# A perceiver kernel whose unit loop goes from three iterations to two, and whose constant rows are filled by transfers

## The chip, the cores and the metric

The kernel runs on one core of one Trainium2 chip, as a single launch. The metric is the device time in microseconds, median of several executions. The engines are named as in the profile: PE (TensorE matmuls) and PEld (its weight loads), DVE (VectorE), ACT (ScalarE), POOL (GpSimd), and SP (SyncE), whose queue issues nearly all DMAs.

## What is computed

The reference is a two-layer perceiver on a latent `x` of 32 batches x 64 tokens x 256, with a context of 32 x 1601 x 256:

```python
x = x + L0_xattn(layernorm(x), ctx, ...)         # 16 heads of 16, 1601 keys
x = x + L0_attn(layernorm(x), ...)               # self-attention over the 64 tokens
x = x + L0_ffn(layernorm(x), ...)                # half of the tokens, chosen by a gate
x = x + L1_xattn(layernorm(x), ctx, mask, ...)   # the same context, masked
x = x + L1_attn(layernorm(x), ...)               # quantized self-attention
x = x + L1_ffn(layernorm(x), ...)                # product-key lookup
```

Each cross-attention projects the whole context to keys and values, takes `softmax(q k^T)` per head, and multiplies by the values. The change concerns the two cross-attentions and the start of the kernel.

## The kernel before, in words

One long part, `stream`, does both cross-attentions and, between them, the small layers of layer 0. The last two layers of layer 1 come behind it and are not touched.

The stream is cut into 256 *units*, `u` = 0 to 255: two layers x 32 batches x four groups of four heads. The order of the instructions on every engine is the order in which the Python code issues them (a manual schedule), so it is written out by hand in the loop of L1408. A unit needs, in this order:

- `fetch(u)` (L1179): the four heads' keys come from a buffer in HBM (`kd`) into one of three SBUF tiles `kst`, by eight DMAs (nine in layer 1, with the mask's row). Numbers are kept as three bf16 parts in different rows of the tile; some rows hold constants: ones at `MAXR`, which -max of the queries multiplies, the mask at `MASKR`, zeros elsewhere. `fetch(u + 2)` is issued at the start of unit `u`, into the tile that unit `u - 1` read last. It also advances the delayed steps (`tick`) by one.
- `maxima(u)` (L1217): scores in natural layout, in four groups of 400 keys: matmuls `sp` (L1228, two PSUM banks a group), DVE's maxima `mx` (L1233); then -max, two small casts `mm`, four matmuls `rp` (L1248) that lay it along the tokens, and two ACT copies (L1253) into the query tile `qst`. It is a generator that stops after each group, after `mm` and after the copies.
- `probabilities(u, j)` (L1259), for seven tiles j of 256 keys (the last has 65): transposed scores less the maximum, matmuls `tp` (L1269), and exp on ACT into a tile `e` (L1274). `tp` has two PSUM banks, `e` has three buffers.
- `weighted(u, j, e)` (L1277): matmuls `acc` (L1284), probabilities times values; each is two instructions, 16 a tile, 8 for the last.

Beside the units run:

- `keys_values` (L1292): projections of later batches, about 1.8 batches ahead, in PSUM banks that alternate between keys (L1081) and values (L1109), twelve matmuls each, some 3.2 banks a unit. DVE adds the key bias into `kr` (L1087); ACT copies values out (L1114).
- `tick` (L997): delayed steps. Each call advances every pending one by one step, with at most two that are marked "work": the split of the context into two parts (`halved`: ACT `chi` L978, then POOL `clo`), the first cast of keys (ACT L1031, then POOL L1032 and L1033), two calls later the second (ACT L1038), then the store to `kd` (L1041, SP).
- `group_step` and `end_step`: one step each of queries, self-attention, the feed-forward layer, and of what follows a finished batch pair.

The before loop has three iterations a unit. With tiles `js` = (0, 1, 2), (3, 4), (5, 6):

```python
for i, js in enumerate(((0, 1, 2), (3, 4), (5, 6))):
    # two steps of maxima(u + 1) in the first and second iteration
    # weighted() of the tiles left from the iteration before
    # in the third: rp and the copies of -max of unit u + 1
    late = [(u, j, probabilities(u, j)) for j in js[:2]]
    # group_step, end_step, tick, then a bank of keys or values
    late += [(u, j, probabilities(u, j)) for j in js[2:]]
```

So -max of a unit is ready before the unit starts. At the start of the kernel, loads of the first context tiles, weights and biases are issued (L1338 on); the key bias's eight small DMAs go on ACT's queue (L268), all others on SP's. POOL sets the constant rows with memsets: two whole `kst` tiles and their rows of ones (L1351 to L1354), two whole `qst` tiles and rows of ones (L1355 to L1362). The first queries follow: DVE's statistics (L561), a small rsqrt on POOL (L199 to L193), normalization on DVE (L568).

Of the kernel before, what the change touches and what calls it, by code (L numbers as in the profile page):

```python
# [20 lines left out]
F32 = mybir.dt.float32  # L21
F32R = mybir.dt.float32r
BF16 = mybir.dt.bfloat16
# [38 lines left out]
class Kernel:  # L62
# [192 lines left out]
    def biases(self, wp, n, which):  # L255
        b = self.WNAMES[n][3]
        got = []
        for x in which:
            full = self.ins[b % x if n else b + x]
            if x == "v":  # L260
                got.append(self.load_row(wp, full, D, f"b{x}{n}"))
            elif x == "k":

                t = wp.tile([P, 2], F32, tag=f"bk{n}", name=f"bk{n}")
                with self.nc.allow_non_contiguous_dma(reason="a bias, once"):
                    for q, a, j in product(range(2), repeat=3):

                        (self.nc.sync if n else self.nc.scalar).dma_start(  # L268
                            t[64 * q + 2 * a + j : 64 * q + 64 : 4],
                            full.rearrange("(c q j a d) -> q j a d c", q=2, j=2, a=2, d=16)[  # L270
                                q, j, a
                            ],
                        )
                got.append(t)
            else:
                got.append(self.load_cols(wp, full, 2, f"b{x}{n}"))
        return got

    def stream_setup(self, wp, bg, bank):
# [41 lines left out]
        tri = bg.tile([P, P], F32, tag="oT", name="tri")  # L321
# [188 lines left out]
    def stream(self):  # L510
        nc, tc, ins = self.nc, self.tc, self.ins
        with ExitStack() as ctx:
# [6 lines left out]
            kq = pool("kq")  # L519
            kp_ = pool("kst")  # L520
            vp_ = pool("v")
            pt = pool("pt", 3)
            small = pool("s", 4)
            work = pool("w", 2)
            bg = pool("bg", 1)
# [72 lines left out]
            def queries(n, g):  # L598

                name = f"xa{n}"  # L600
                if g == 0 and n == 1:
                    self.load_natural(self.wq, ins[self.WNAMES[n][0]])
                xT = yield from normed(g, name)
                qp = project(None, self.wq, xT, f"{name}_qp{g}")
                qf = bg.tile([P, 2, 2 * P], F32, tag="qf", name=f"{name}_qf{g}")
                for oc in range(2):
                    nc.vector.tensor_scalar(
                        qf[:, oc, :], qp[:, oc, :], self.bq[n][:, oc : oc + 1],
                        0.25 if n else 1.0, ALU.add, ALU.mult,
                    )  # L610
# [12 lines left out]
                waiting[0] = True  # L623
                yield
                yield
                q = qring[g % 2]
                qh = halves(q)
                for a in range(2):
                    for r, rows, part in (
                        (a, FIRST, 0), (1 - a, FIRST, 2), (a, SECOND, 1), (1 - a, SECOND, 0),  # L630
                        (a, THIRD, 0), (1 - a, THIRD, 1),
                    ):
                        nc.sync.dma_start(
                            parity(qh[r, rows], a),
                            qd[part].rearrange("(j a d) n -> a d j n", a=2, d=16)[a],
                        )
                        if r != a:
                            yield

                nc.sync.dma_start(q[MAXR : P : 64], q[ZERO : P : 64])  # L640
                qsts[NG * n + g] = q
                yield

# [154 lines left out]
            def self0(g):  # L798
                xT = yield from normed(g, "sa0")
                rp = bank(f"sa0_rp{g}")  # L800
                for cc in range(2):
# [28 lines left out]
                def out(t, oT):  # L830
                    rp = bank(f"sa0_ro{g}_{t}")
                    for c in range(2):
                        nc.tensor.matmul(
                            rp[:NH, :P], self.basT[:, c, 3 * NH :], oT[:, c, :],
                            start=(c == 0), stop=(c == 1),
                        )
                    ro = bg.tile([NH, P], F32, tag="ro", name=f"sa0_rs{g}_{t}")
# [10 lines left out]
            def ffn0(g):  # L848
# [12 lines left out]

                def wide(tag, dt=F32):

                    home = dict(dg="oT", row="ro").get(tag, f"ff_{tag}")
                    return bg.tile([P, 2, NQ], dt, tag=home, name=f"ff0_{tag}{g}")


# [156 lines left out]
            def parted(i, x, quick):  # L1024
# [9 lines left out]
                if not quick:  # L1034

                    yield "wait"
                    yield "work"
                nc.scalar.copy(ks[:, 1, :, :m], upper(x))  # L1038
                yield "store"
                for b, k0, n, o in spans(i):  # L1040
                    nc.sync.dma_start(  # L1041
# [307 lines left out]


            for k in kring[:2]:  # L1351
                nc.gpsimd.memset(k, 0.0)
                for r in (MAXR, MAXR + 64):
                    nc.gpsimd.memset(k[r : r + 1], 1.0)  # L1354
            for q in qring:  # L1355
                nc.gpsimd.memset(q, 0.0)

                for a in range(2):
                    r = 64 * a + 32
                    nc.gpsimd.memset(  # L1360
                        q[r : r + 5].rearrange("p (j a) n -> p j a n", a=2)[:, :, a], 1.0
                    )  # L1362
# [4 lines left out]
            for i in range(6):  # L1367
# [4 lines left out]
            pad = bg.tile([P, 6, NKP - NK], BF16, tag="e", name="pad")  # L1372
            nc.vector.memset(pad, 0.0)
            nc.sync.dma_start(self.rows[:, NK:], pad[:NB, 0])

            for kd in kdring:
                nc.sync.dma_start(
                    kd.rearrange("s (c q) (h n) -> (q h) (s c) n", c=2, h=4)[:, :, NKE:],
                    pad[:, :, : NKP - NKE],
                )  # L1380
            steps = queries(0, 0)

# [17 lines left out]
            fetch(1)  # L1400
            banks_made(3)
            LEAD = 1.8
            for i, _ in enumerate(maxima(0)):
                if i < 4:
                    banks_made(1)
            groups.append((15, self.stream_setup(wp, bg, bank)))
            late = []
            for u in range(NU):  # L1408
# [14 lines left out]
                    groups.append((u + 15, queries(*divmod((u + 15) // 16, NG))))  # L1423
                if u + 2 < NU and u + 2 not in ksts:
                    fetch(u + 2)
                nat = maxima(u + 1) if u + 1 < NU else iter(())

                for i, js in enumerate(((0, 1, 2), (3, 4), (5, 6))):
                    for _ in range((2, 2, 0)[i]):
                        next(nat, None)  # L1430
                    for done in late:
                        weighted(*done)
                        if done[1] == 6 and done[0] % 8 == 7:
                            n, t = divmod(done[0] // 8, NT)
                            ends.append((n, t, finish(n, t)))
                            next(ends[-1][2])
                    if i == 2:
                        next(nat, None)
# [7 lines left out]
                    if i == 2:  # L1446
                        group_step()
                        if u % 2:
                            end_step()
                for _ in nat:  # L1450
                    pass
            for done in late:
                weighted(*done)
            ends.append((1, NT - 1, finish(1, NT - 1)))
# [973 lines left out]
```

## Time and profile before

| | |
|---|---|
| median of 3 executions | 3675.83 us (3670.55 to 3685.44) |
| the profiled execution | 3673.05 us |
| its span, first to last instruction | 3671.3 us |
| mean granted PE clock | 0.953 |
| first maxima matmul (unit 1's first) | 99.22 us (113.46 us) |
| last unit's first `acc` of its own tiles | 3134.24 us |
| PE waiting for DMA of `kst`, 300 to 3100 us | 16.2 us keys, 13.9 us mask rows |
| PE `acc` waiting for ACT `e`, 300 to 3100 us | 6.9 us |

The span is measured by the profiler; the device time of the same execution stands beside it. In a line of the timeline the columns are: start in us, duration, engine, line of the kernel, operation, tiles written and read, shapes, how many instructions were merged (x12), and in brackets how long the engine was idle before and what ended that. Matmuls overlap, so the time of a run of them is read from its start to the start of the next run. In a line of the waits: who waited, for whom, us in total, times, longest.

### The profile page before, as it was taken

The page shows a single profiled execution, that of the slowest core. Times are in us where ns is not written, and L with a number is a line of the kernel's source. Part 1 is how long each engine was busy: PE and PEld are TensorE (multiplying, and loading weights), DVE is VectorE, ACT ScalarE, POOL GpSimd, SP SyncE. Part 2 cuts the span into 40 slices and gives each one's busy share as a digit, 9 for nine tenths or more (in the row PEclk, how much of TensorE's full clock was granted, in tenths as well). Part 3 has the DMA queues.
Part 4 walks back from the last instruction along what each step waited for, and adds up shares of the span by engine and source line. Part 5 has one row for each costly group of instructions (what it writes and reads, how often), then busy time and mean ns, then how long its engine had stood idle before and what let it go on. Part 6 is the DMA issues. An engine that isn't in the chain of part 4 may idle for free. (4 is left out here: it accounts for less than half of the span.)

```text
span 3671.3 us, 148311 instructions
## 1 busy us (share of the span) xinstructions
PE 3325.6 (91%) x62993; PEld 2715.0 (74%) x63007; DVE 2430.4 (66%) x6165; ACT 2367.4 (64%) x4656; POOL 1837.9 (50%) x2121
## 2 busy tenths in 40 slices
PE   3799999999999999999999999999999998675698
PEld 3688788878778788778887878878788887332467
DVE  5556566666565566566567666656666666689879
ACT  2567666766766677667776767667677776154662
POOL 6455555554555555545555655555565563003246
PEclk9899999999999999999999999999999999886699
DMA  3888777776776777677787677677778887100000
GB/s 83 227 230 235 200 195 208 216 210 191 212 198 189 210 202 217 189 204 209 204 219 217 190 207 202 191 210 195 207 205 239 233 236 208 64 1 1 1 5 20
DMA packets 615336, 649.81 MB, mean 177 GB/s; under 512 B 127056, under 2 KB 579856, under 8 KB 598096
## 3 DMA queue, kind: packets, MB, share of 16 engines
q1 hardware_dynamic: 614288, 640.31, 63.5%
q8 instruction: 495, 8.11, 0.9%
q14 instruction: 169, 1.38, 0.1%
q10 hardware_dynamic: 384, 0.00, 0.0%
HBM read 468.30 MB, written 171.11 MB: 174 GB/s over the span
## 5 line engine op out<-in xcount | busy, mean ns | idle before, releaser
L1233 DVE TENSOR_REDUCE mx<-sp 128x1 f32<-128x400 f32 (+1 forms) x2048 | 1032.2, 566 | 314.1 <-PE sp L1228 313.6
L1274 ACT ACTIVATE e<-tp 128x512 f32<-128x512 f32 (+1 forms) x1792 | 931.7, 565 | 472.7 <-PE tp L1269 463.2
L979 POOL TENSOR_TENSOR clo<-raw,chi 128x512 fp32r<-128x512 f32 (+1 forms) x408 | 507.8, 1245 | 550.4 <-ACT chi L978 539.1
L1032 POOL TENSOR_TENSOR kr<-kr,ks 128x512 f32<-128x512 f32 (+1 forms) x406 | 459.0, 1130 | 620.9 <-ACT ks L1031 563.5
L1087 DVE TENSOR_SCALAR kr<-kp,bk 128x256 f32<-128x256 f32 (+1 forms) x832 | 356.5, 470 | 552.9 <-PE kp L1081 455.9
L1269 PE MATMUL tp<-qst,kst 128*128 128x64 bf16 (+1 forms) x13312 | 580.2, 195 | 18.3 <-ACT e L1274 15.9
L1284 PEld LDWEIGHTS acc<-e,v 128*17 128x17 f32 x26624 | 397.3, 98 | 217.7 <-issue 141.8
L1284 PE MATMUL acc<-e,v 128*17 128x64 f32 x26624 | 543.8, 223 | 14.7 <-ACT e L1274 11.5
L1269 PEld LDWEIGHTS <-kst 128*128 128x128 bf16 (+1 forms) x13312 | 463.1, 100 | 118.2 <-issue 25.7
L1109 PE MATMUL vp<-w_hi,chi 128*128 128x256 f32 (+1 forms) x1664 | 508.5, 306 | 33.2 <-DVE w_hi L222 30.0
L1109 PE MATMUL vp<-w_lo,chi 128*128 128x256 f32 (+1 forms) x1664 | 473.8, 285 | 0.4 <-DVE w_lo L223 0.3
L1109 PE MATMUL vp<-w_hi,clo 128*128 128x256 f32 (+1 forms) x1664 | 474.1, 285 | 0.0
L1033 POOL TENSOR_TENSOR ks<-kr 128x512 bf16<-128x512 f32 (+1 forms) x406 | 412.5, 1016 | 31.9
L1081 PE MATMUL kp<-chi,w_hi 128*128 128x256 f32 (+1 forms) x1664 | 370.8, 305 | 22.6 <-DVE w_hi L222 19.8
L1228 PE MATMUL sp<-kst,qst 64*64 64x400 bf16 (+1 forms) x4096 | 321.4, 351 | 76.6 <-DMA kst<-kd 39.2
L1114 ACT COPY v<-vp 128x512 f32<-128x512 f32 (+1 forms) x416 | 244.8, 589 | 206.5 <-PE vp L1109 203.4
L1081 PE MATMUL kp<-clo,w_hi 128*128 128x256 f32 (+1 forms) x1664 | 339.4, 286 | 16.5 <-POOL clo L979 15.6
L1109 PEld LDWEIGHTS vp<-w_hi,chi 128*128 128x128 f32 (+1 forms) x1664 | 314.4, 189 | 51.1 <-DVE w_hi L222 26.9
L1081 PE MATMUL kp<-chi,w_lo 128*128 128x256 f32 (+1 forms) x1664 | 337.1, 285 | 4.8 <-DVE w_lo L223 4.8
L1109 PEld LDWEIGHTS vp<-w_lo,chi 128*128 128x128 f32 (+1 forms) x1664 | 314.9, 189 | 1.7 <-DVE w_lo L223 0.9
L1109 PEld LDWEIGHTS vp<-w_hi,clo 128*128 128x128 f32 (+1 forms) x1664 | 314.2, 189 | 0.0
L978 ACT CAST chi<-raw 128x512 fp32r<-128x512 f32 (+1 forms) x410 | 249.7, 609 | 86.7 <-DMA raw<-in_ctx_dram 86.6
(725 smaller groups left out, 5191.5 us busy)
## 6 DMA issues: line engine op xcount, KB each, us to landing
kst<-kd SPq DMA_DIRECT2D x1024, 208.0 KB
kd<-ks SPq DMA_DIRECT2D x384, 384.0 KB
kst<-kd SPq DMA_DIRECT2D x1024, 104.0 KB
raw<-in_ctx_dram SPq DMA_DIRECT2D x379, 256.0 KB
qst<-xa_qd SPq DMA_DIRECT2D x192, 64.0 KB
kd<-ks SPq DMA_DIRECT2D x64, 108.0 KB
xa_qd<-xa_qs SPq DMA_DIRECT2D x16, 384.0 KB
raw<-in_ctx_dram SPq DMA_DIRECT2D x62, 72.0 KB
```

Of the source, the lines that this page charges most:

```text
L978: nc.scalar.copy(hi[:, :, :n], raw[:, :, :n])
L979: (nc.vector if i < 2 else nc.gpsimd).tensor_tensor(lo[:, :, :n], raw[:, :, :n], hi[:, :, :n].bitcast(F32), ALU.subtract)
L1032: eng.tensor_tensor(x, x, ks[:, 0, :, :m], ALU.subtract)
L1033: eng.tensor_tensor(ks[:, 2, :, :m], x, upper(x), ALU.subtract)
L1081: nc.tensor.matmul(kp[:, oc, :m], wk[w][:, cc, oc * P : (oc + 1) * P], x[:, cc, :m], start=(j == 0), stop=(j == 5),)
L1087: nc.vector.tensor_scalar(r[:, oc, :m], kp[:, oc, :m], self.bk[n][:, oc : oc + 1], None, ALU.add,)
L1109: nc.tensor.matmul(vp[:w_, i1, :], x[:, cc, o], wv[w][:, cc, :], start=(j == 0), stop=(j == 5),)
L1228: nc.tensor.matmul(sp[a][64 * j : 64 * j + 64, :n], q[r, h0 + 2 * j + a, tok], k[r, 2 * a + j, k0 : k0 + n], start=True, stop=True,)
L1233: nc.vector.tensor_reduce(mx[:, a, g : g + 1], sp[a][:, :n], AX.X, ALU.max)
L1269: nc.tensor.matmul(sp[:m, c, h, :], k[:, 2 * (h % 2) + h // 2, k0 : k0 + m], q[:, h0 + h, tok], start=True, stop=True,)
L1274: nc.scalar.activation(e[:m, :two], sp[:m, :two], AF.Exp)
L1284: nc.tensor.matmul(acc[32 * h : 32 * h + 17, slot, :], vs[b, c][:m, 4 * q4 + h, :], e[:m, c - 2 * i, h, :], start=(c == 0), stop=(c == NCH ...
```

## The change

The loop now has two iterations a unit. `maxima(u + 1)` does two of its steps in each; what is left of it, `rp` and the copies of -max, is kept as `own` and done in the first iteration of the unit that uses it, with a bank of keys or values between it and the unit's first scores. Tiles go out as 0, 1, then 2, 3 in the first iteration, 4, 5, 6 in the second, with banks between; `weighted` runs on four tiles (0 to 3) and three (4 to 6), so `e` has four buffers. `group_step`, `end_step` and `tick` (together `behind()`) are called four times a unit. In `parted`, the store of keys comes one tick later. To make room for the fourth buffer, the tiles `oT` and `ro` share buffers with others. At the start, the memsets of POOL are gone; a small tile of zeros and ones (`flat`) is written into the constant rows by ten DMAs on SP's queue, and the key bias's DMAs go on SP's queue too, behind the query weights. The rows of the query tiles that multiply the mask are zeros in layer 0, and are set to ones by two DMAs for the first two query groups of layer 1; the copy of zeros over the -max row is left out for the first two groups.

```diff
-                        (self.nc.sync if n else self.nc.scalar).dma_start(
+                        self.nc.sync.dma_start(
...
-            pt = pool("pt", 3)
+            pt = pool("pt", 4)
...
-                nc.sync.dma_start(q[MAXR : P : 64], q[ZERO : P : 64])
+                if n or g > 1:
+                    nc.sync.dma_start(q[MAXR : P : 64], q[ZERO : P : 64])
+                if n and g < 2:
+                    for a in range(2):
+                        r = MASKR + 64 * a
+                        nc.sync.dma_start(
+                            parity(q[r : r + 1], a),
+                            kring[0][MAXR : MAXR + 1, 0:1, : 2 * P].to_broadcast([1, 8, 2 * P]),
+                        )
...
-                rT = bg.tile([3 * NH, 2 * P], F32, tag="oT", name=f"sa0_rT{g}")
+                rT = bg.tile([3 * NH, 2 * P], F32, tag="kz", name=f"sa0_rT{g}")
...
                 nc.scalar.copy(ks[:, 1, :, :m], upper(x))
+                if not quick:
+                    yield "wait"
                 yield "store"
...
-            self.bk = self.biases(wp, 0, "k")
...
-            self.bq, self.bv = self.biases(wp, 0, "q"), []
+            self.bk, self.bq, self.bv = self.biases(wp, 0, "k"), self.biases(wp, 0, "q"), []
...
-            for k in kring[:2]:
-                nc.gpsimd.memset(k, 0.0)
-                for r in (MAXR, MAXR + 64):
-                    nc.gpsimd.memset(k[r : r + 1], 1.0)
-            for q in qring:
-                nc.gpsimd.memset(q, 0.0)
...
+            flat = bg.tile([P, 2, 512], BF16, tag="fraw", name="flat")
+            for x in range(2):
+                nc.vector.memset(flat[:, x], float(x))
+            def fill(rows, x):
+                rows = rows.rearrange("p h n -> p (h n)").rearrange("p (x n) -> p x n", n=512)
+                nc.sync.dma_start(
+                    rows, flat[: rows.shape[0], x : x + 1].to_broadcast(list(rows.shape))
+                )
+            for x in kring[:2] + qring:
+                for r in (32, 96):
+                    fill(x[r : r + 32 : 2], 0)
+            for k in kring[:2]:
+                fill(k[MAXR : P : 64], 1)
...
-                nat = maxima(u + 1) if u + 1 < NU else iter(())
-                for i, js in enumerate(((0, 1, 2), (3, 4), (5, 6))):
-                    for _ in range((2, 2, 0)[i]):
+                nat, own = maxima(u + 1) if u + 1 < NU else iter(()), nat
+                def some(*js):
+                    late.extend((u, j, probabilities(u, j)) for j in js)
+                def behind():
+                    banks[0] = 0
+                    group_step()
+                    end_step()
+                    tick()
+                def made_up_to(part):
+                    keys_values(LEAD + (u + part) / 4.0, 0.15)
+                for i in range(2):
+                    for _ in range(2):
                         next(nat, None)
                     for done in late:
                         weighted(*done)
...
-                    late = [(u, j, probabilities(u, j)) for j in js[:2]]
-                    banks[0] = 0
-                    group_step()
-                    end_step()
-                    tick()
-                    keys_values(LEAD + (3 * u + i + 1) / 12.0, 0.15)
-                    late += [(u, j, probabilities(u, j)) for j in js[2:]]
...
+                    late = []
+                    if i == 0:
+                        next(own)
+                        behind()
+                        made_up_to(1 / 3.25)
+                        some(0, 1)
+                        behind()
+                        made_up_to(2 / 3.25)
+                        some(2, 3)
+                    else:
+                        behind()
+                        some(4)
+                        made_up_to(1.0)
+                        some(5)
+                        behind()
+                        some(6)
```

More of the change, by code (lines that the diff above doesn't have):

```diff
@@ L320, in stream_setup @@
         nc.vector.tensor_tensor(self.eye, self.ident[:, :64], self.ident[:, 64:], ALU.add)
-        tri = bg.tile([P, P], F32, tag="oT", name="tri")
+        tri = bg.tile([P, P], F32, tag="e", name="tri")
         nc.gpsimd.memset(tri, 1.0)
@@ L836, in out @@
                         )
-                    ro = bg.tile([NH, P], F32, tag="ro", name=f"sa0_rs{g}_{t}")
+                    ro = bg.tile([NH, P], F32, tag="xT", name=f"sa0_rs{g}_{t}")
                     nc.scalar.copy(ro, rp[:NH, :P])
@@ L862, in wide @@
                 def wide(tag, dt=F32):
-                    home = dict(dg="oT", row="ro").get(tag, f"ff_{tag}")
+                    home = dict(dg="kz", row="kT").get(tag, f"ff_{tag}")
                     return bg.tile([P, 2, NQ], dt, tag=home, name=f"ff0_{tag}{g}")
@@ L1345, in stream @@
             self.load_natural(self.wq, ins[self.WNAMES[0][0]])
-            self.bq, self.bv = self.biases(wp, 0, "q"), []
+            self.bk, self.bq, self.bv = self.biases(wp, 0, "k"), self.biases(wp, 0, "q"), []
             kring = [kp_.tile([P, 4, NKP], BF16, tag=f"kst{r}", name=f"kst{r}") for r in range(3)]
             qring = [kq.tile([P, 16, 2 * P], BF16, tag=f"qst{r}", name=f"qst{r}") for r in range(2)]
-            for k in kring[:2]:
-                nc.gpsimd.memset(k, 0.0)
-                for r in (MAXR, MAXR + 64):
-                    nc.gpsimd.memset(k[r : r + 1], 1.0)
-            for q in qring:
[L1356 to L1362, printed above, removed]
             kdring = [
@@ L1371, in stream @@
                 )
-            pad = bg.tile([P, 6, NKP - NK], BF16, tag="e", name="pad")
-            nc.vector.memset(pad, 0.0)
-            nc.sync.dma_start(self.rows[:, NK:], pad[:NB, 0])
+            flat = bg.tile([P, 2, 512], BF16, tag="fraw", name="flat")
[11 more added lines that the diff above has]
+                fill(k[MAXR : P : 64], 1)
+            nc.sync.dma_start(self.rows[:, NK:], flat[:NB, 0, : NKP - NK])
+            pad = flat[:, 0, : 6 * (NKP - NKE)].rearrange("p (x n) -> p x n", x=6)
             for kd in kdring:
@@ L1378, in stream @@
                     kd.rearrange("s (c q) (h n) -> (q h) (s c) n", c=2, h=4)[:, :, NKE:],
-                    pad[:, :, : NKP - NKE],
+                    pad,
                 )
@@ L1402, in stream @@
             LEAD = 1.8
-            for i, _ in enumerate(maxima(0)):
-                if i < 4:
-                    banks_made(1)
+            nat = maxima(0)
+            for _ in range(4):
+                next(nat)
+                banks_made(1)
             groups.append((15, self.stream_setup(wp, bg, bank)))
@@ L1436, in stream @@
                             next(ends[-1][2])
-                    if i == 2:
-                        next(nat, None)
-                    late = [(u, j, probabilities(u, j)) for j in js[:2]]
-                    banks[0] = 0
-                    group_step()
-                    end_step()
-                    tick()
-                    keys_values(LEAD + (3 * u + i + 1) / 12.0, 0.15)
-                    late += [(u, j, probabilities(u, j)) for j in js[2:]]
[L1446 to L1451, printed above, removed]
+                    late = []
[14 more added lines that the diff above has]
+                        some(6)
             for done in late:
```

## The prediction

> **What bounds the kernel now.** I read the page's busy shares and slices first, then busy time by stretch, then the timelines of the start and of one unit, last the waits of PE and of SP's queue.
>
> ```profile
> PE 3325.6 (91%) x62993; PEld 2715.0 (74%) x63007; DVE 2430.4 (66%) x6165; ACT 2367.4 (64%) x4656; POOL 1837.9 (50%) x2121
> PE   3799999999999999999999999999999998675698
> PEclk9899999999999999999999999999999999886699
> ```
> ```profile
> 0.00:40.00 40.00, 3.27 (x12) 2.71 (x12) 21.48 (x17) 3.66 (x5) 39.09 (x33) 1.00 0.41 101
> 40.00:80.00 40.00, 23.53 (x159) 22.41 (x160) 16.18 (x28) 11.70 (x22) 20.81 (x19) 1.00 0.20 56
> ...
> 1100.00:1500.00 400.00, 388.46 (x7874) 323.39 (x7866) 246.46 (x595) 277.98 (x569) 206.44 (x220) 0.99 0.73 201
> 1500.00:1900.00 400.00, 382.86 (x7688) 321.60 (x7688) 249.54 (x607) 275.12 (x562) 207.65 (x224) 0.97 0.76 207
> ```
> Columns of the second: stretch, its length, busy PE, PEld, DVE, ACT, POOL, clock, DMA share, GB/s. From about 95 to 3105 us, where the 256 units run, PE is busy 96 to 97% and nothing else over 73%: a microsecond on PE is a microsecond of the kernel. Two things can be won there: the idle 3 to 4%, and dead time that counts as busy where one kind of matmul follows another. In the first 80 us PE is idle two thirds of the time.
>
> The Trainium skill (Perfetto Trace Analysis, Identifying the Most-Contended Engine) calls matmul busy time a poor measure and asks for the weight loads' share. Those are busy 74%, so by the page a quarter of PE would be headroom.
>
> I price PE by the starts of its runs, which leave the switches below and no more.
>
> **The start (memsets to transfers): -33 us.**
> ```profile
> 25.32 11.31 POOL L1354 MEMSET kst<- 1x6656 bf16 x2
> 36.69 3.52 POOL L1356 MEMSET qst<- 128x4096 bf16 x1
> ...
> 51.25 0.24 POOL L199 TENSOR_SCALAR xa_rs_v<-xa_mv 128x2 f32<-128x2 f32 x1
> ...
> 53.44 0.73 DVE L568 TENSOR_SCALAR xa_xn<-X,xa_mv,xa_rs_y 128x256 f32<-128x256 f32 x2 [21.42 <-POOL xa_rs_y L193]
> ```
> POOL fills from 2.5 to 51.2; the small rsqrt of the first queries is queued behind it, DVE waits 21.42 us for that, and the split of the value weights, next on DVE at 54.09, releases PE at 54.56. With the fills gone, DVE's statistics would be followed at once. The first `kr` add (27.96 before) now waits for the key bias: its eight DMAs go on SP after the query weights' issue (6.01 + 0.37); eight such issues at L268 took 5.60 later in this trace, so the last goes out at about 11.3 and lands at about 14 (2.6 us, as the mask fetch issued at 3120.97 released PE at 3123.58). From that add to the first value matmul were 54.56 - 27.96 = 26.6 us, 19.2 of them the wait for POOL (51.25 less 32.02, the end of the statistics): 7.4 remain, so values start at 21.4, 33 us earlier. Bounds: 38 if the bias is no wait; 22 if the ten fill DMAs (about 0.6 us of SP issue each, 6 us) and 1.4 MB of them delay key stores and fetches behind them on SP. The fills themselves are needed only at the first maxima, 99 us before. Whatever PE gains here stays, as PE is full after it.
>
> The Trainium skill (DMA: Bandwidth & Descriptors, Issuing engines are not separate DMA queues) says that queues share the same 16 DMA engines and that a second queue saves issue time only; by it moving the bias costs those 5.6 us of issue and nothing else.
>
> **Fewer runs on PE: -38 us.** One unit's PE rows:
> ```profile
> 1343.24 0.53 PE L1284 MATMUL acc<-e,v 128*17 128x64 f32 x24
> 1343.70 0.64 PE L1269 MATMUL tp<-qst,kst 128*128 128x64 bf16 x16
> 1347.05 0.41 PE L1269 MATMUL tp<-qst,kst 128*128 128x64 bf16 x8
> 1347.39 0.54 PE L1228 MATMUL sp<-kst,qst 64*64 64x400 bf16 x8
> 1347.85 0.86 PE L1284 MATMUL acc<-e,v 128*17 128x64 f32 x48
> 1348.65 0.64 PE L1269 MATMUL tp<-qst,kst 128*128 128x64 bf16 x16
> ```
> Start to start: 24 `acc` take 0.46, 48 take 0.80, so one takes 0.0142 and leaving `acc` for `tp` costs 0.12. A value bank followed by `acc` lasts 1.61 (1611.69 to 1613.30), followed by `tp` 1.50 (1619.29 to 1620.79): entering costs 0.10. Before has three `acc` runs a unit (24, 48, 32), after two (40, 64): 0.22 less. Two `sp` runs, four `tp` runs and 3.2 key/value banks stay. -max is now followed by a bank with its 128-column loads; four such matmuls then `tp` took 0.22 (1351.19 to 1351.41), so the new switch costs between 0 and 0.15 more; I take 0.07, the middle, as both are 128-column loads. 0.15 x 256 = 38 (18 to 56).
>
> **exp of the last tile: +149 us.** This is the term that decides. ACT works in order:
> ```profile
> 1656.78 0.59 ACT L1114 COPY v<-vp 128x512 f32<-128x512 f32 x1 [0.99 <-PE vp L1109]
> 1657.27 0.60 ACT L1274 ACTIVATE e<-tp 128x512 f32<-128x512 f32 x1
> 1658.78 1.09 ACT L1274 ACTIVATE e<-tp 128x512 f32<-128x512 f32 x2 [0.91 <-PE tp L1269]
> 1659.75 0.62 ACT L1038 COPY ks<-kr 128x512 bf16<-128x512 bf16 x1
> 1660.26 0.63 ACT L978 CAST chi<-raw 128x512 fp32r<-128x512 f32 x1
> ```
> Each such operation costs 0.5 of pitch. Before, tiles 5 and 6 go out ahead of `tick`, and a bank of 1.4 us stands between them and their `acc`: both have time. After, tile 5 follows the unit's last bank, then come `group_step`, `end_step` and `tick` with up to two copies, and only then tile 6; its `acc` is the third of the next unit, with no bank between.
> - PE, from the first matmul of tile 5: 0.25 for it, 0.12 for tile 6, 0.09 to `sp` (1347.05 to 1347.39 less eight at 0.031), 0.46 of `sp`, 0.46 for the `acc` of tiles 4 and 5: tile 6 is wanted at 1.38.
> - ACT: exp 5 starts at 0.51 after a key bank (1631.92 to 1632.43) or 0.68 after a value bank, whose copy comes first (1656.59 to 1657.27); then 0.49, 0.5 for each copy of the tick, and 0.37 for tile 6: 1.37 or 1.54, plus 0.5 per copy.
> - Copies: after a key bank its first cast, and the second cast of the key bank two ticks back: two; after a value bank the next `chi`: one.
>
> So PE waits 1.0 or 0.7 us, 0.83 on average, where no group step gives PE work there; about half of the iterations have some, 0.4 us on the mean, with ACT copies of its own. I take 0.6. The last seven units have no banks: 249 x 0.6 = 149 us. Bounds: 0.1 (group work, and copies that fall on other ticks) and 1.0: 25 to 249. Tile 3 has a whole bank ahead of it, as tile 2 has now, and costs nothing.
>
> **Key fetches and stores: -25 us.**
> ```profile
> SPq L1041 <- ACT ks L1038: 261.9, 110, 7.7
> SPq L1195 <- PE tp L1269: 202.1, 114, 6.9
> ```
> SP stands 261.9 us at key stores that wait for ACT, with fetches queued behind; PE waits 16.2 + 13.9 us for fetched keys and mask rows between 300 and 3100. The extra `yield "wait"` puts the store one tick later, when the copy is done. Against it, tile 6 is now the unit's last work, so the fetch that overwrites those keys starts about 1.5 us later. I take -25; bounds -30 and +60 (below).
>
> **The rest: +6 us.** In the last units no bank covers the copies of -max (0.74) ahead of the first scores: 0.9 x 7. Fourth exp tile, shared buffers, skipped zero copies for the first queries and mask rows set by DMA for layer 1: nothing, beside a full PE; a shared buffer that made group steps wait would cost some 0.5 us in each of 64 attention steps, 30 us, which I leave to the upper end.
>
> **Sum.** 3673.05 (span 3671.3 and 1.75 around it) - 33 - 38 - 25 + 149 + 6 = 3732. The median of before lies 2.8 above its profiled execution: **3735**.
>
> A clock effect is not in it. From 3080 to 3130 the granted clock is 0.83, though PE waits no longer than 1.63 us at a time there; the steady stretches have 0.97 to 0.99. If waits of a microsecond in each unit cost a point of clock, that is 28 us of 2800, kept for the upper end. The Trainium skill (TensorE: Matmul & The Clock Gate, HAM oscillation) has the clock fall only for gaps beyond about 3.4 us; by it the new waits cost none.
>
> **Rivals.**
> - *Faster: exp keeps up* (0.30). If group work and other ticks cover tile 6 (0.1 us a unit), 25 replaces 149: 3735 - 124 = 3611. For it: ACT is busy only 70%; half the iterations have group work. Against: ACT's total doesn't matter, its order in 1.4 us does. It tips at 0.36 us a unit (90 us).
> - *No change: fetches become the bound* (0.14). In the tail a fetch first issued at 3115.12 released PE at 3123.58, 8.5 us; a unit without group work then leaves it one unit time, some 9.2 us. If a third of the units are late by 0.9, +77 stands in place of -25; with exp covered, 3673 - 33 - 38 + 77 + 6 + 3 = 3688.
> - *Forecast* (0.52), exp of the last tile late. The remaining 0.04: the clock or shared buffers on top, 3790 and beyond.
>
> Under 0.5% (18 us, about what a measurement here can tell from no change): faster 0.30, same 0.15, slower 0.55. Range 3595 to 3790: it reaches down to the first rival with the larger switch saving, and up to waits of 0.8.
>
> **What would show it.** Start: first value matmul near 21 us, no POOL memset of `kst`. Switches: two `acc` runs of 40 and 64. The deciding row: PE `acc` waiting for ACT `e`, about 150 us in total (before 6.9 from 300 to 3100). SP's wait for L1038's successor nearly gone. I am wrong if that `acc` wait stays under 60 us, or if the starts of the units are set by DMA of `kst`.

## The result, and the profile after

| | before | after |
|---|---|---|
| median | 3674.95 us (4 executions, 3670.55 to 3685.44) | 3812.17 us (4 executions, 3805.54 to 3815.87) |
| profiled execution, its span | 3673.05, 3671.3 us | 3805.54, 3803.8 us |
| mean granted PE clock | 0.953 | 0.948 |

After over before is 1.037, 95% interval 1.034 to 1.039: 137 us slower. The forecast was 3735, slower; the time lies above its range of 3595 to 3790.

The page's first two parts, of the changed kernel:

```profile
PE 3346.3 (88%) x62993; PEld 2746.9 (72%) x63007; DVE 2457.7 (65%) x6166; ACT 2370.2 (62%) x4656; POOL 1792.2 (47%) x2109
...
PE   6899999999999899998999989989989898684688
PEclk8899999999999999999999999999999999886699
```

Every engine but POOL has the busy time of before within 1.2%. The work is the same. Of the 132.5 us of span that have come in, 111.8 are idle time on PE and 20.7 are busy time, for the same number of matmuls. The same stretches as before, of the changed kernel (stretch, length, busy PE, PEld, DVE, ACT, POOL, clock, DMA share, GB/s):

```profile
0.00:40.00 40.00, 20.82 (x132) 19.42 (x132) 16.46 (x37) 10.55 (x17) 9.78 (x37) 0.87 0.79 148
40.00:80.00 40.00, 26.59 (x168) 23.24 (x169) 21.46 (x36) 16.30 (x31) 9.80 (x9) 0.75 0.72 201
...
1100.00:1500.00 400.00, 371.34 (x7495) 313.47 (x7493) 248.44 (x593) 265.74 (x541) 201.37 (x214) 0.99 0.72 197
1500.00:1900.00 400.00, 362.14 (x7118) 304.87 (x7117) 253.68 (x597) 253.17 (x519) 194.57 (x217) 0.95 0.69 188
```

In the first 40 us PE is busy 20.82 us where it was 3.27, while the DMA engines went from 0.41 to 0.79. In the steady stretches PE has lost 17 to 21 us in 400. Who ended those waits, from 300 to 3100 us (us in total, times, longest):

```profile
PE acc L1295 <- ACT e L1285: 149.9, 187, 4.5
PE sp L1239 <- DMA kst<-kd: 12.6, 12, 3.0
PE tp L1280 <- ACT e L1285: 10.4, 19, 1.1
PE sp L1239 <- DMA kst<-rows: 10.3, 5, 3.7
```

The first line before was

```profile
PE acc L1284 <- ACT e L1274: 6.9, 5, 3.5
```

That is the row that the prediction named. That its value agrees ("about 150 us") is in part luck: the row counts only what PE stood idle between 300 and 3100 us. By the start times of the matmuls, below, tile 6 alone costs 0.82 us a unit, 204 us in 249 units, where 149 were forecast. What SP's queue waits for, whole run:

```profile
SPq L1206 <- PE sp L1239: 717.9, 192, 12.8
...
SPq L1206 <- DMA kd<-ks: 118.8, 53, 4.3
```

The stand of 261.9 us at the key stores is gone; SP stands instead at the fetches, for the unit that still reads the tile. PE's waits for `kst` went from 30.1 to 22.9 us only: SP's queue waits longer and PE hardly notices.

One end of a unit, on PE and on ACT:

```profile
1617.25 0.41 PE L1280 MATMUL tp<-qst,kst 128*128 128x64 bf16 x8
1617.49 0.42 PE L673 MATMUL xa_oT<-ident,xa_raw 128*128 128x128 f32 x2
1617.74 0.29 PE L1280 MATMUL tp<-qst,kst 128*65 128x64 bf16 x4
1617.97 0.54 PE L1239 MATMUL sp<-kst,qst 64*64 64x401 bf16 x8
1618.43 0.64 PE L1295 MATMUL acc<-e,v 128*17 128x64 f32 x32
1620.15 0.30 PE L1295 MATMUL acc<-e,v 65*17 65x64 f32 x8 [1.08 <-ACT e L1285]
```
```profile
1617.44 0.59 ACT L1125 COPY v<-vp 128x512 f32<-128x512 f32 x1 [0.73 <-PE vp L1120]
1617.93 0.60 ACT L1285 ACTIVATE e<-tp 128x512 f32<-128x512 f32 x1
1618.41 0.38 ACT L675 COPY xa_raw<-xa_oT 128x256 f32<-128x256 f32 x1
1618.67 0.64 ACT L1046 COPY ks<-kr 128x512 bf16<-128x512 bf16 x1
1619.19 0.64 ACT L986 CAST chi<-raw 128x512 fp32r<-128x512 f32 x1
1619.70 0.39 ACT L1285 ACTIVATE e<-tp 65x256 f32<-65x256 f32 x1
```

Read them together. Tile 5's scores start on PE at 1617.25 and its exp on ACT at 1617.93, after the value copy. Tile 6's four scores are done at about 1618.0, but three operations stand ahead of its exp on ACT: one of a group step, two of the tick. It starts at 1619.70, ends at 1620.09, and the eight `acc` that need it start at 1620.15, 1.08 us idle. ACT is never late in total (62% busy); the last operation of the unit is simply last in its line.

**Where the 132.5 us stand**, by the starts of the units' first `tp` on PE: unit 2 comes at 120.1 for 143.9 (-23.8); from there to unit 240, 2998.3 for 2849.4 (+148.9); from unit 240 to the last `tp` +7.2; the tail behind +0.3. Per unit, from the start times of PE's matmuls in units 50 to 239: 12.66 us for 12.00. The time within the `acc` runs rose from 1.49 to 2.47, all the rest fell from 10.51 to 10.19. Tile 6's first `acc` starts 0.86 us on the mean after the `acc` before it, where 0.04 is the rule; tile 3's 0.14. (An `acc` run is a row of `acc` matmuls with no other matmul between.)

### The profile page after: what moved, and what is told of

Its sections match the earlier page's. It is cut to its first block, busy times and chain, and to the rows that moved or that the text cites. A ratio compares the mean times of both kernels' runs of the same rounds, so it can differ in the third digit from the quotient of the medians.

```text
span 3803.8 us, 148330 instructions
## 1 busy us (share of the span) xinstructions
PE 3346.3 (88%) x62993; PEld 2746.9 (72%) x63007; DVE 2457.7 (65%) x6166; ACT 2370.2 (62%) x4656; POOL 1792.2 (47%) x2109
## 5 line engine op out<-in xcount | busy, mean ns | idle before, releaser
L1285 ACT ACTIVATE e<-tp 128x512 f32<-128x512 f32 (+1 forms) x1792 | 962.0, 569 | 445.5 <-PE tp L1280 443.7
L1295 PE MATMUL acc<-e,v 128*17 128x64 f32 x26624 | 563.1, 222 | 182.3 <-ACT e L1285 175.9
L1280 PE MATMUL tp<-qst,kst 128*128 128x64 bf16 (+1 forms) x13312 | 602.7, 195 | 35.5 <-ACT e L1285 19.7
L1280 PEld LDWEIGHTS <-kst 128*128 128x128 bf16 (+1 forms) x13312 | 485.0, 100 | 120.6 <-issue 64.7
L1239 PE MATMUL sp<-kst,qst 64*64 64x400 bf16 (+1 forms) x4096 | 294.1, 346 | 47.2 <-DMA kst<-kd 24.1
L1039 ACT CAST ks<-kr 128x512 bf16<-128x512 f32 (+1 forms) x416 | 253.6, 610 | 61.4 <-DMA kd<-ks 42.7
```

Source lines behind the costliest of these rows:

```text
L1039: nc.scalar.copy(ks[:, 0, :, :m], x)
L1239: nc.tensor.matmul(sp[a][64 * j : 64 * j + 64, :n], q[r, h0 + 2 * j + a, tok], k[r, 2 * a + j, k0 : k0 + n], start=True, stop=True,)
L1280: nc.tensor.matmul(sp[:m, c, h, :], k[:, 2 * (h % 2) + h // 2, k0 : k0 + m], q[:, h0 + h, tok], start=True, stop=True,)
L1285: nc.scalar.activation(e[:m, :two], sp[:m, :two], AF.Exp)
L1295: nc.tensor.matmul(acc[32 * h : 32 * h + 17, slot, :], vs[b, c][:m, 4 * q4 + h, :], e[:m, c - 2 * i, h, :], start=(c == 0), stop=(c == NCH ...
```

## The experiments

Ratios are to the kernel before on the same chip, with 95% intervals. Waits of PE are from 300 to 3100 us.

**Tile 6 ahead of the delayed steps.**
```diff
-                        some(5)
-                        behind()
-                        some(6)
+                        some(5, 6)
+                        behind()
```


> Only change against the changed kernel: tile 6's scores and exp are issued right after tile 5's, ahead of group_step, end_step and tick. Theory (exp of tile 6 stands behind other ACT operations, 0.82 us of stall a unit on the mean): the acc wait for e, 157.6 us between 300 and 3250, falls under 40 us, and the time by about 0.75 x 249 = 190 us, to some 3620 us; 3600 to 3650. Rival (the stall is the bank that is missing between a unit's last scores and its last acc, so any order of ACT is late): exp 6 then comes only 0.5 us behind exp 5, the wait stays above 100 us and the time above 3740. Rival (two iterations cost as such, by waits of -max or of fetches): the acc wait goes and another takes its place, time above 3740.

Measured: 3694.09 us, 1.007 (1.0048 to 1.0091); from 1.037 that is 0.030, or 109 us. The wait of `acc` for `e` is no longer among the first rows:

```profile
PE tp L1280 <- ACT qst L1264: 27.3, 45, 2.1
PE tp L1280 <- ACT e L1285: 22.2, 29, 2.3
PE sp L1239 <- DMA kst<-kd: 19.2, 22, 2.8
PE sp L1239 <- DMA kst<-rows: 15.8, 9, 2.7
```

The mechanism stands: the order on ACT made the wait, and the rival that blamed the missing bank is out. But some 190 us were expected and 109 came, so the other rival, that another wait takes the place, is right in part. Within the `acc` runs 0.82 us a unit went, as expected; elsewhere 0.35 came back. Waits for -max's copies (`qst`) rose from 4.4 to 27.3 us, those for `kst` from 22.9 to 35.0. The waits of `tp` for `e` rose from 10.4 to 22.2. While PE stood 0.82 us for tile 6, keys and copies caught up beside it. These rows make 47 of the some 85 us that came back; the rest wasn't traced.

**Only the tick behind tile 6.**
```diff
-                        behind()
-                        some(6)
+                        banks[0] = 0
+                        group_step()
+                        end_step()
+                        some(6)
+                        tick()
```


> Against the changed kernel, of the three steps ahead of tile 6 only tick goes behind it; group_step and end_step stay ahead. Theory (about 1.5 of the 2.1 ACT operations between exp 5 and exp 6 are copies of the tick, 0.5 us each): 0.6 to 0.75 us a unit go, 150 to 185 us, time 3625 to 3665, and the rest of the acc wait (30 to 60 us) falls in units with a group step. Rival (the group's own ACT copies and the PE work that they wait for are the larger part): less than 75 us go, time above 3735.

Measured: 3699.88 us, 1.0086 (1.0062 to 1.011), nearly all that the first run gained. The time misses the expected 3625 to 3665 for the same reason as there. The `acc` wait fell to 7.4 us (300 to 3150), where 30 to 60 were expected to stay: the tick's copies made the lateness. With a group step alone ahead of it tile 6's `acc` is 0.04 us late on the mean.

**The loop alone and the start alone.** The first has the memsets and bias queue of before with the new loop; the second the fills, the bias queue and the shared buffers with the old loop, three `e` buffers and the old store step.

> The changed loop, store step, shared buffers and four exp tiles, with the memsets and the bias queue of before at the start. Theory (the parts add up; the start is worth 24 to 28 us by the starts of units 0 and 2): 3812 + 24 to 28 = 3836 to 3840 us. Rival (the first key fetches and not the start are what the start gave back to; then the start is worth the 33 us of the first value matmul): 3845 or more. Rival (the loop gains from a slower start nothing, the start is worth nothing at the end): 3812.

> The fills by transfers, the key bias on SP's queue and the shared buffers, with the loop, three exp tiles and store step of before. Theory (part of the 36 us that the first value matmul gains is given back to the fills on SP's queue and the DMA engines before unit 2): 24 to 28 us faster than before, 3647 to 3651. Forecast as it was on record: 33 faster, 3642. Rival (nothing of it reaches the end): 3675.

Measured: loop alone 3838.10, 1.0465 (1.0443 to 1.0487); start alone 3643.76, 0.9934 (0.9913 to 0.9956). The parts add up within their intervals: the start is worth 24 us by the second (16 to 32), 36 by the difference of the first to the whole change, whose interval reaches down to 23. In the start-alone trace unit 2 comes 32 us earlier (111.6). A part is given back on SP, as its rows show:

```profile
13.52 6.03 SPq L1372 DMA_DIRECT2D kst<-flat  x4
19.59 6.71 SPq L1372 DMA_DIRECT2D qst<-flat  x4
26.41 2.03 SPq L1372 DMA_DIRECT2D kst<-flat  x2
...
33.12 0.51 SPq L1049 DMA_DIRECT2D kd<-ks  x1
```

The first key store goes out at 33.12, behind the fills. ACT then waits until 38.83 for it (5.69 us), the context split behind that comes late, and PE stands 4.19 us, until 41.87.

**One exp more, before and after.** An extra exp of 128x512 on ACT ahead of tile 6's exp in each unit, its result overwritten.
```diff
+                if i == 6:
+                    nc.scalar.activation(e, tps[0], AF.Exp)
                 nc.scalar.activation(e[:m, :two], sp[:m, :two], AF.Exp)
+                tps[0] = sp
```


> The kernel before with one extra exp of 128x512 on ACT in front of tile 6's exp in every unit; its result is overwritten. Theory (only what stands between a tile's scores and its acc counts; before, tile 6's exp ends 2.24 us ahead of its acc on the mean): 0.5 us more on ACT costs nothing, 3668 to 3680. Rival (ACT's load in all, 0.5 us a unit, reaches the end of the kernel): 3790.

> The changed kernel with the same extra exp in front of tile 6's exp. Theory (here the last exp is on the path in nearly every unit): 0.49 x 249 = 122 us more, 3935 (3915 to 3945), and the acc wait for e rises by as much. Rival (the wait is for something else that exp only ends last beside, such as a free buffer or group work): under 60 more, below 3875.

Measured: in the kernel before 3703.29, 1.0072 (1.0053 to 1.0091), 26 us; in the changed kernel 3950.53, 1.0757 (1.0728 to 1.0785), 0.039 or 143 us more than without it, 6 us above the expected range; in the trace 128 us = 0.50 x 256. There the wait rises by 107 us:

```profile
PE acc L1300 <- ACT e L1289: 256.8, 208, 5.0
```

The same half microsecond costs its full price where the operation is last in line and a fifth of it where tile 6 has 2.24 us to spare. There it was expected to be free (3668 to 3680) and isn't quite: in the trace of before with it, that `acc` wait stays low (4.8 us), but other rows rise (`sp` waiting for mask rows, 21.0 for 13.9, and for a value copy, 5.4 for 1.1).

**Tiles 0 to 2, then 3 to 6** ("tiles 3 + 4" below, by their number in each iteration). With tile 6 cured, tiles 2 and 3 are the next late ones.
```diff
-                        some(2, 3)
+                        some(2)
                     else:
-                        behind()
-                        some(4)
-                        made_up_to(1.0)
-                        some(5)
-                        behind()
-                        some(6)
+                        some(3, 4)
+                        behind()
+                        made_up_to(1.0)
+                        some(5, 6)
+                        behind()
```


> Two iterations as in the changed kernel, but tiles 0 to 2 in the first and 3 to 6 in the second, with tiles 2, 5 and 6 right behind a bank and behind() only after tile 6. Theory (with tile 6 cured, tiles 2 and 3 are the next late ones: the 102 starts within the acc runs still take 1.65 us a unit in the run with tile 6 first, 1.46 in the kernel with only the start changed): these starts fall to about 1.50, the time by 0.15 x 256 = 38 us below 3694, to some 3655 (3640 to 3670). Rival (the rest comes from -max and its copies in front of the first scores, which this kernel leaves where they are): 3680 to 3700.

Measured: 3669.86, 0.9984 (0.9971 to 0.9998), 32 us below the run with tile 6 first. The size came, its reason only in part: the `acc` starts take 1.62 us a unit, not 1.50. Tile 3 is in time, but tile 2 now starts 0.19 us after the `acc` before it; the rest fell at changes from one kind of matmul to the next (2.59 to 2.52 us) and in `tp` (1.55 to 1.51).

**The store step by itself**, on the start alone.

> The kernel with only the start changed, plus the key store one tick later. Theory as on record (SP's stand of 256 us at the stores holds up fetches, and PE's waits for keys and mask rows, 50 us between 300 and 3150, come from it): about 25 us below 3644, so 3620. Rival (those waits come from the fetches' own place behind the last scores of the unit that still reads the tile): SP's wait for ACT's ks goes, PE's waits for kst stay, 3640 to 3648.

Measured: 3660.42, 0.9957 (0.9942 to 0.9973), no gain over the start alone (0.9934). SP's queue, whole run:

```profile
SPq L1052 <- ACT ks L1046: 217.4, 90, 7.5
SPq L1206 <- PE tp L1280: 201.4, 107, 6.3
```

Neither case held: the wait that the store step was meant to end stayed, 217.4 for 256.2 us, and PE's waits for `kst` fell from 50.0 to 37.8 us without a gain in time. Another wait of PE rose by more than that; it was 10.1 us without the store step:

```profile
PE tp L1280 <- ACT e L1285: 30.2, 26, 4.4
```

In the changed kernel, then, the new order of the loop must have had a part in moving SP's waiting.

**-max in another place.** Its four matmuls `rp` and two copies go ahead of the two groups of `sp` and the `acc`, in three versions of the loop: tile 6 first, tiles 3 + 4, and that one with a `behind()` moved to stand after tile 2.
```diff
+                next(own)
                 for i in range(2):
                     for _ in range(2):
                         next(nat, None)
...
-                        next(own)
```


> The kernel with tile 6 first, and -max of the unit (rp and its two copies) moved ahead of the two groups of sp and the acc that come before it. Theory (what is left of the loss, 0.23 us a unit against the kernel with only the start changed, is for two thirds -max in front of the first scores: 0.15 us waiting for its copies, 0.12 of more waits around rp): PE's wait of tp for qst, 32.3 us, goes, and with the waits around rp 30 to 55 us in all; ratio to before 0.992 to 0.999. Rival (the loss is in tiles 2 and 3 and in the fetches): 1.004 to 1.010, as with tile 6 first alone.

> The same move of -max in the kernel with tiles 0 to 2 and 3 to 6. Theory (the two cures add): 30 to 55 us below that kernel, ratio to before 0.983 to 0.990. Rival: 0.996 to 1.000, as before the move.

> As the run before, and the behind() that stood between tile 1 and the second bank goes behind tile 2, so that its matmuls cover exp of tile 2, now late by 0.15 us a unit. Theory: up to 0.15 x 256 = 38 us less, half of it if only units with group work gain; ratio to before 0.974 to 0.985. Rival (the copies of the tick, now ahead of tiles 3 and 4, or the two banks in a row without a step between them cost as much): as the run before.

Measured: 1.042 (1.0397 to 1.0443), 1.0286 (1.026 to 1.0312), 1.0417 (1.0393 to 1.044). Gains were expected. The first two lost 0.035 and 0.030 against the same loops without the move, and the third lost 0.013 against the second. Waits of the first of them:

```profile
PE kp L1092 <- ACT qst L1264: 37.7, 26, 3.3
PE tp L1280 <- ACT qst L1264: 16.1, 24, 2.5
...
PE vp L1120 <- ACT qst L1264: 9.0, 11, 1.5
```

All waits of PE for -max's copies come to 103 us, 76 more than with tile 6 first, out of 128 us that the move cost; most are not at the scores that need -max but at whatever comes next (`kp`, `vp`, group steps). The code says why that can be: `sp`, `rp`, keys, values and group steps take the five PSUM banks of `psm` in turn. `rp` holds one until its copies are done, and these stand on ACT behind two exps and the tick; two groups of `sp` use the four others, and the next taker waits. In the third version `tp` waits 83.9 us for `e` as well (300 to 3150).

Two more runs tell bank and ACT's order apart: `rp` behind `sp` and ahead of `acc`, with tile 6 first and with tiles 3 + 4.

> The kernel with tile 6 first, and -max's four matmuls and two copies between the two groups of sp and the acc behind them. Theory A (what made -max ahead of sp so dear, 1.042 against 1.007, was its PSUM bank: the two groups of sp and the next bank go round the five banks and come to those that wait for ACT; behind sp that is gone, and the 40 acc cover the copies): faster than with tile 6 first alone, 1.000 to 1.004. Theory B (not the bank but ACT's order: the copies of the tick stand ahead of -max's copies, and exp of tile 0 behind them): as bad as ahead of sp for half of it, 1.02 or more. Rival (no effect): 1.005 to 1.009.

> The same place of -max in the kernel with tiles 0 to 2 and 3 to 6 (0.9984). Theory A: 0.990 to 0.995, level with the kernel with only the start changed (0.9934). Theory B: 1.01 or more. Rival (no effect): 0.997 to 1.000.

Measured: 1.0076 (1.0055 to 1.0098) and 1.0028 (1.0013 to 1.0042), for 1.007 and 0.9984 without the move. So the loss of the earlier place is gone, as the bank theory has it. Theory B is out, since the order on ACT is the same in both places. But theory A's gain didn't come: the first run fits the rival of no effect, and the second is 0.004 slower than without the move. In the first of the two the waits for `qst` stay at 24.3 us (27.3 before the move), and `rp` itself now waits 52.8 us (9.1 before the move), 37.9 of them for DVE, which empties banks that come ahead of it in the same turn:

```profile
PE rp L1259 <- DVE kr L1098: 14.2, 38, 1.1
PE rp L1259 <- DVE ff_e L751: 9.5, 8, 1.2
PE rp L1259 <- DVE sa_e L751: 8.2, 8, 1.2
```

**The fills on POOL's queue**, with the old loop.
```diff
-                nc.sync.dma_start(
+                nc.gpsimd.dma_start(
                     rows, flat[: rows.shape[0], x : x + 1].to_broadcast(list(rows.shape))
                 )
```


> The kernel with only the start changed, with the ten fills on POOL's queue in place of SP's. Theory (the fills hold SP's queue from 13.5 to 28.4 us, so the first key store goes out at 33.1 and ACT waits 5.7 us for it; the part of the start's gain that is lost is issue on SP): the first key store goes out some 15 us earlier, that wait goes, unit 2's first tp comes 4 to 8 us before 111.6, ratio 0.990 to 0.993. Rival (the DMA engines, 0.84 to 0.93 busy from 10 to 40 us, are what is full): unit 2 within 2 us of 111.6.

Measured: 3653.56, 0.9945 (0.9925 to 0.9966), no better than on SP's queue; unit 2 at 121.1, 9.5 us later than there. DVE and PE at its start:

```profile
23.75 0.88 DVE L1095 TENSOR_SCALAR kr<-kp,bk 128x256 f32<-128x256 f32 x2 [13.94 <-DMA bk<-in_L_xattn_bk_dram]
```
```profile
31.23 0.58 PE L1117 MATMUL vp<-w_hi,chi 128*128 128x256 f32 x1 [22.21 <-DVE w_hi L222]
```

The fills went out from 2.5 us on, and the DMA engines were busy 0.80 and 0.91 in the first two stretches of 10 us. SP took far longer to issue the key bias's eight DMAs than in the kernel with only the start changed (first line; here the second):

```profile
3.86 5.33 SPq L267 DMA_DIRECT2D bk<-in_L_xattn_bk_dram  x8
```
```profile
3.89 18.26 SPq L267 DMA_DIRECT2D bk<-in_L_xattn_bk_dram  x8
```

So the bias released DVE at 23.75 where it had done so at 10.92, the first value matmul comes at 31.23 for 18.38, and the first key store goes out at 30.80, 2.3 us earlier and not 15. ACT's wait for that store is gone, as expected, and still nothing is won. Neither case has its number: the rival is right that another queue doesn't help, but unit 2 is 9.5 us late where it allowed 2. Early fills push away what is needed first. The Trainium skill (DMA: Bandwidth & Descriptors, Issuing engines are not separate DMA queues) says that transfers from any engine share the same 16 DMA engines; this run agrees, in that fills issued by POOL held up SP's bias by 13 us.

## Why the prediction was wrong, by its own steps

The sign, the deciding term and its row were right. The total was not: 59 us forecast, 132.5 in the profiled executions.

- **Start, -33:** right in kind, 9 us too large. The first value matmul came at 18.35 (forecast 21.4), but unit 2 only 23.8 us earlier, and 32 with the old loop. The lower gain of 22 named a cause, fills ahead of key stores on SP's issue and in the DMA engines. The rows of the start alone fit it; which of the two counts isn't settled, as the fills on POOL's queue slowed SP's issue as well.
- **Fewer runs, -38:** right in kind, a little small. Changes from one kind of matmul to the next (all group work as one kind), without the recorded idle, take 1.95 us a unit for 2.19, and 2.03 with tile 6 first: 0.24 and 0.16 saved, where 0.15 was forecast. The first is 61 us in 256 units, above the bound of 56.
- **exp of the last tile, +149: this is the step that failed, by its size.** "I take 0.6" was 0.82 for tile 6, 204 us in 249 units. The price of a copy was near: in units 50 to 239, where only copies of the tick stand between exp 5 and exp 6, one makes tile 6 late by 0.54 us and two by 1.00 (0.7 and 1.0 were forecast). What failed is the discount of 0.23 for group work. The 70 units with an operation of a group step in that line are late by 0.78 us, the 120 without by 0.85. Group work does give PE something to do, but its own copies stand in the same line ahead of exp 6. The count was low too: 1.68 copies of the tick on the mean for 1.5, and 0.39 operations of group steps, 2.07 in all (one in 41 units, two in 99, three in 45, four in 5).
- **"Tile 3 ... costs nothing"** failed too. A bank stands ahead of tiles 2 and 3, but none between them and their `acc`. Tile 3's `acc` start 0.10 us late and tile 5's 0.04; tile 2's 0.06, which were 0.07 late before. Together the `acc` runs grew by 0.98 us a unit where 0.60 was forecast, and all else fell by 0.32 where 0.25 was. The 0.38 over some 240 units is 91 us, more than the whole miss of 73.
- **Fetches and stores, -25:** failed. SP's wait of 261.9 us was read as PE's loss. It did go, and PE's waits for `kst` fell by 7 us. (That nothing but PE was over 73% overlooks the DMA engines' 0.76 in the same rows; it didn't bear on the result.) The store step alone brought no gain (0.9957 for 0.9934).
- **Rest, +6:** the wait was right, the sum wasn't. In each of the last seven units `tp` waits 0.83 us for -max's copies (0.9 forecast). Yet units 248 to 255 together take only 0.2 us more than before; of the +7.2 behind unit 240, 7.0 lie in units 240 to 247. With tile 6 cured, `tp` waits for these copies 45 times between 300 and 3100 us too, 27.3 us in all, where banks are there to cover them. The shared buffers, which the kernel with only the start changed also has, cost nothing that shows.
- **Clock:** the 28 us kept for it were too many. From 300 to 3050 us the mean granted clock is 0.978 for 0.983. If all of that is PE's time, it is an estimated 14 us; but one other trace without such waits, only the tick behind tile 6, has 0.978 too, so the difference isn't clear of the spread.
- **Rivals:** that exp keeps up is out by 149.9 us of waits; that fetches bound the units is out by 22.9 us.

The experiments give a second account, by what each cure is worth. Each ratio in it is good to about 0.002. The new loop costs 0.043 of the time at the same start (1.037 less 0.9934), 159 us. The place of tile 6 is 0.030 of it, the places of tiles 2 and 3 some 0.009, and 0.005, about 18 us, is left. In the left part lie the saved runs and, against them, waits for -max (24.5 us with tiles 3 + 4, none with the old loop) and the store step, which the old loop was run without; how the rest divides wasn't settled. Tile 6 by this account is 109 us, while 0.82 us x 249 = 204 us stood at its `acc`: the rest of that stand hid other waits. Which of the two numbers is "the cost of tile 6" depends on the question, and a prediction that adds up terms needs to say that the waits behind are not in it.

No version of the two-iteration loop that was tried beats the old loop with the new start, which is the fastest kernel here by its median: 3643.76 us, 0.9934.

## What to carry to other kernels

When a loop is shortened, write down for each in-order engine what stands between an operand's producer and its consumer, with the delayed steps counted from the trace and not from the mean load: here 62% busy ACT cost 0.8 us a unit by order alone. A wait of a queue's issuer is not a loss until the engine that bounds the kernel is shown to wait for it. And a stall can be longer than what its removal gives, since other waits stand behind it: here 204 us gave 109.

## What the runs showed of the hardware

- Short waits can lower the granted clock a little. From 300 to 3050 us its mean is 0.983 in the kernel before, 0.978 in the changed one and 0.968 with one exp more, the lowest of all traces here (the others 0.976 to 0.986); it falls to half for 96, 123 and 174 us in all. PE stands longer than 3.4 us only five, five and two times there. The Trainium skill (TensorE: Matmul & The Clock Gate, HAM oscillation) has the rule of no gaps beyond about 3.4 us; these traces don't agree with it as a limit. In the kernel before, the clock is 0.51 from 641.3 to 644.7 us, with PE busy throughout and no wait over 2.1 us in the 7 us ahead; with one exp more it is 0.50 from 1134.3 to 1137.7 us, with none over 1.6 us in the 7 us ahead.
- A PSUM bank that waits for its copy stops the users that come after it in turn. With -max's four tiny matmuls ahead of two groups of `sp` (0.46 us of matmuls) and not behind them, the kernel took 1.042 for 1.0076 at the same order on ACT, and `kp` stood 37.7 us for copies into `qst`, which it doesn't read.
- Ten fill transfers took 15 us of issue on SP, and the first key store behind them landed 5 to 6 us after its issue, with the DMA engines 0.93 busy from 30 to 40 us. With the same ten on POOL's queue, eight bias DMAs took 18.26 us of issue on SP for 5.33, and the bias came 13 us later.
